# Per-type node sums ahead of the weights, in half blocks, in a graph layer on one core

## The chip, the cores and the metric

The kernel runs on one core of one Trainium2 chip. The metric is the device time of one execution in microseconds (us), and the time given for a kernel is the median of its runs. A core has a matrix engine (TensorE), a vector engine (VectorE), a scalar engine (ScalarE), GpSimd, and SyncE, which here only starts transfers. Each runs its own instruction list in order; semaphores order them against each other.

## The reference

There are 6250 nodes with 128 features, and 100000 edges sorted by destination. Each edge takes its source's row of x through one of two weight matrices, chosen by the edge's type, and the results are summed by destination. A third matrix acts on the node's own row. Then come relu, the residual and a layer norm.

```python
Xs = X[src]
m_data = Xs @ W_data.T + b_data
m_ctrl = Xs @ W_control.T + b_control
msg = jnp.where((edge_types == 0)[:, None], m_data, m_ctrl)
agg = jax.ops.segment_sum(msg, dst, num_segments=X.shape[0])
out = agg + (X @ W_self.T + b_self)
x = _layernorm(x + jax.nn.relu(out), axis=-1)
```

All is fp32. The kernel holds fp32 numbers as three bf16 parts that add up to them, so 128 features are 384 bf16 columns (`D3`).

## The kernel before

**Blocks.** The nodes are cut into 49 blocks of 128 (`NB`). For each block the kernel loads a window of 18 x 128 edges (`KT`, `WIN`), which holds all edges that end in the block. A count of matched edges at the end decides whether a slow general path (`sums_over_all`) has to run; with these inputs it doesn't.

**Messages first.** In a first stage x (transposed, from `in_xt`) is split in three bf16 parts (`split_x`), multiplied by the two type weights (`multiply`, `y`, full-width matmuls), and the fp32 result is split again into three parts: `take` copies a part from the sums to `m3` on ScalarE, `leave` subtracts it on TensorE with minus the unit matrix. `m3` holds 98 tiles of 128 messages, one for each block and type. It stays in the core and is also written to `table` in memory.

**40 packed blocks** in 8 groups of 5 (`GROUPS`) are summed without indirect loads. For a group:

- `edge_fields` computes for each edge its source tile, its place in the tile and its destination; `bucket_hots` makes one-hot rows over the 98 source tiles (`hot_st`); `ranks` counts with `tri` and `rest` matmuls into `acc` and VectorE reductions (`slot`), one step after the other over 18 steps, which of 32 slots (`R`) of its source tile an edge takes.
- `fill_a` and `fill_b` write source and destination of each slot into `small` by matmuls; `fill_c` packs them (`vs`, `packed`) and builds the list of edges that found no slot ("over" to "spilled"), whose messages are fetched with an indirect load (`msg_s`).
- For each block `spread` loads the packed slots to all partitions (`rows`), `select` compares them with the partition number, and `to_hots` makes the one-hot of destinations (`hot_d`).

Then, for each of 25 tiles of four source tiles (`NS`), `gather` runs four matmuls that pick 32 messages each into `g_ps`, `evict` copies them to `gs` on ScalarE, and `add_up` adds them into the block's sum `agg`, again with four matmuls of 32 columns of weights (`by_columns`): each writes its own 32 output partitions. `own_of` adds the node's own term, from x parts that the first stage wrote to memory (`x3_t`) and `load_own` reads back.

**9 gathered blocks** are summed from indirect loads of 128 messages (`gather_rows`, `msg`), 18 per block, beside the packed ones (`gathered_sums`, `agg_g`).

**Behind the sums** `finish_blocks` adds the three parts (`whole`), relu and residual and the statistics, and `normalise` ends a group.

**The order** of all instructions on all engines comes from a planner in the kernel (`Order`): each function is a stream of named steps with an engine, an assumed cost and the steps it needs; `due` gives each a due time, and the planner repeatedly takes the step that can start first, by due time among near ones. The order is then fixed in each engine's instruction list.

Of the kernel before, what the change touches and what calls it, by code (L numbers as in the profile page):

```python
# [26 lines left out]
NT = 2 * NB  # L27
KT = 18
WIN = KT * P
EC = 125  # L30
ER = E // EC
EPS = 1e-05

GROUPS = (5,) * 8
# [6 lines left out]
NS = (NT + 3) // 4  # L41
NC = 4 * NS
# [4 lines left out]
PARTS = (4, 8, 8, 8, 8, 8, 5)  # L47
CH = 6
KC = 6
DC = 13  # L50
# [54 lines left out]
def kernel(  # L105
# [28 lines left out]

    nc = tc.nc
    dram = ctx.enter_context(tc.tile_pool(name="dram", bufs=1, space=DRAM))
    const = ctx.enter_context(tc.tile_pool(name="const", bufs=1))
    table = dram.tile([NT * P, D3], BF16, name="table")
    x3_t = dram.tile([NB, D, 3 * P], BF16, name="x3_t")
    packed = dram.tile([NPB, NT * R], BF16, name="packed")  # L140
    total = const.tile([1, 1], I32, name="total")

    def finish(h, agg, xs):

        nc.vector.scalar_tensor_tensor(h, agg, 0.0, xs, op0=ALU.max, op1=ALU.add)

    def add_parts(agg, work):
        whole = work.tile([P, D], F32, name="whole")
        nc.vector.tensor_reduce(whole, agg.rearrange("p (i c) -> p c i", i=3), axis=AX.X, op=ALU.add)  # L149
        return whole  # L150

    def load_rows(b, work, name="xs", bufs=2):
        xs = work.tile([P, D], F32, name=name, bufs=bufs)
        nc.sync.dma_start(xs, x[b * P : (b + 1) * P, :])
        return xs
# [46 lines left out]
    with ExitStack() as main:  # L202
        sums_over_windows(main, tc, x, xt, edges, w, bias, table, x3_t, packed, total,
                          add_parts, finish, load_rows, norm)

    matched = nc.values_load(total[0:1, 0:1])
    with tc.If(matched != E), ExitStack() as rest:
        sums_over_all(rest, tc, xt, edges, w, bias, table, dram, finish, load_rows, norm)


def sums_over_windows(ctx, tc, x, xt, edges, w, bias, table, x3_t, packed, total,
                      add_parts, finish, load_rows, norm):
# [4 lines left out]
    own_pool = ctx.enter_context(tc.tile_pool(name="own_pool", bufs=1))  # L217
    row_pool = ctx.enter_context(tc.tile_pool(name="row_pool", bufs=RB))
    ps_a = ctx.enter_context(tc.tile_pool(name="ps_a", bufs=1, space=PSUM))
    ctx.enter_context(tc.manual_schedule())  # L220
    stats, root, scale, apply, store_out = norm
    order = Order()
    YB = 4
# [7 lines left out]
    r0 = const.tile([EC, 1], I32, name="r0")  # L231
    nc.sync.dma_start(r0, edges.rearrange("(p k) c -> p (k c)", p=EC)[:, 1:2])
    early = ctx.enter_context(ExitStack())
    build = early.enter_context(tc.tile_pool(name="build", bufs=2))
    ps_y = early.enter_context(tc.tile_pool(name="ps_y", bufs=YB, space=PSUM))
    w_sb = build.tile([D, D3], F32, name="w_sb", bufs=1)
    A.dma_start(w_sb, w)
    b1 = build.tile([1, D3], F32, name="b1", bufs=1)
    A.dma_start(b1, bias)


    iota_f = const.tile([P, 640], F32, name="iota_f")
    G.iota(iota_f, pattern=[[1, 640]], base=0, channel_multiplier=0,
# [4 lines left out]
    base = const.tile([P, NB], I32, name="base")  # L248
    G.iota(base, pattern=[[P, NB]], base=0, channel_multiplier=0)
    counted = {}  # L250
    for n in sorted({DC, CH, *GROUPS}):
        counted[n] = const.tile([P, P, n], BF16, name=f"count{n}")
        G.iota(counted[n], pattern=[[1, P], [0, n]], base=0, channel_multiplier=0,
               allow_small_or_imprecise_dtypes=True)
    bound_p = const.tile([NB, 1], F32, name="bound_p")
    V.tensor_scalar_mul(bound_p, pid[:NB], float(P))
    bound_f = const.tile([EC, NB], F32, name="bound_f")
    V.tensor_scalar_mul(bound_f, iota_f[:EC, :NB], float(P))
    pid1 = const.tile([P, 1], F32, name="pid1")
    V.tensor_scalar_add(pid1, pid, 1.0)  # L260
    slot_f = const.tile([P, R], F32, name="slot_f")
    V.tensor_scalar_add(slot_f, iota_f[:, :R], SLOT)
    ones = const.tile([P, P], F32, name="ones")
# [3 lines left out]
    ident = const.tile([P, P], F32, name="ident")  # L267
    V.tensor_scalar(ident, iota_f[:, :P], pid, None, op0=ALU.is_equal)


    r0f = work.tile([EC, 1], F32, name="r0f")
    V.tensor_copy(r0f, r0)
    begun = work.tile([EC, NB], F32, name="begun")
    V.tensor_scalar(begun, bound_f, r0f, None, op0=ALU.is_gt)
    row_ps = ps_a.tile([P, 512], F32, name="small")
    T.matmul(row_ps[:NB, 0:1], begun, ones[:EC, 0:1], start=True, stop=True)
    row_f = work.tile([NB, 1], F32, name="row_f")
    V.tensor_scalar(row_f, row_ps[:NB, 0:1], -1.0, 0.0, op0=ALU.add, op1=ALU.max)
    row_i = work.tile([NB, 1], I32, name="row_i")
    V.tensor_copy(row_i, row_f)  # L280

    er = build.tile([NB, ER, 3], I32, name="er", bufs=1)
    G.indirect_dma_start(
        out=er.rearrange("p k c -> p (k c)"), out_offset=None,
        in_=edges.rearrange("(p k) c -> p (k c)", p=EC),
# [3 lines left out]
    def three_parts(parts, whole, left):  # L289

        V.tensor_copy(parts[0], whole)
        V.tensor_sub(left, whole, parts[0])
        V.tensor_copy(parts[1], left)
        V.tensor_sub(parts[2], left, parts[1])

    w3 = const.tile([D, 3, D3], BF16, name="w3")
    left = build.tile([D, D3], F32, name="left", bufs=1)
    three_parts([w3[:, i, :] for i in range(3)], w_sb, left)
    order.free["V"] = 7.3


    minus = const.tile([P, P], BF16, name="minus")
    bias3 = const.tile([P, 2 * D], BF16, name="bias3")
# [3 lines left out]
    spill_tiles = [(const.tile([P, Q * P], BF16, name=f"hot_s{i}"),  # L307
                    const.tile([P, D3], BF16, name=f"msg_s{i}")) for i in range(2)]
    hot_b = const.tile([P, P], BF16, name="hot_b")
    msg_b = const.tile([P, D3], BF16, name="msg_b")  # L310
    slot_values = [const.tile([P, (Q + 1) // 2, NC], BF16, name=f"vs{i}") for i in range(2)]
    slot_b = {n: const.tile([P, R, n], BF16, name=f"slot{n}") for n in sorted({*GROUPS})}

    def constants():
        yield step("bias", {"V": 2.4}, ("xr", 0))
        V.memset(bias3, 0.0)
        parts = build.tile([1, 3, D3], BF16, name="parts", bufs=1)
        three_parts([parts[:, i, :] for i in range(3)], b1, left[:1])
        V.tensor_scalar_mul(minus, ident, -1.0)
        yield step("biased", {"A": 1.2}, "bias")  # L320
        for i in range(3):
            A.copy(bias3[32 * i : 32 * i + 1, :], parts[0:1, i, : 2 * D])

        yield step("set", {"V": 4.0}, "bias")
        tri_f = build.tile([P, P], F32, name="tri_f", bufs=1)
        V.tensor_scalar(tri_f, iota_f[:, :P], pid, None, op0=ALU.is_gt)
        V.scalar_tensor_tensor(tri_f, ident, SLOT, tri_f, op0=ALU.mult, op1=ALU.add)
        V.tensor_copy(tri, tri_f)
        V.tensor_scalar(rest, tri_f, -1.0, 1.0, op0=ALU.mult, op1=ALU.add)
        V.tensor_copy(ident_b, ident)  # L330
        for n, tile_n in slot_b.items():
            V.tensor_scalar_add(tile_n, counted[n][:, :R, :], SLOT)


        for vs in slot_values:
            V.memset(vs, 255.0)


        for hot, msg in [*spill_tiles, (hot_b, msg_b)]:
            V.memset(hot, 0.0)  # L340
            V.memset(hot[R : R + 1, :], 1.0)
            V.memset(msg, 0.0)
            V.tensor_copy(msg[R : R + 1, :].rearrange("p (i c) -> p i c", i=3),
                          parts[0:1, :, 2 * D :])

    win, win_g = {}, const.tile([P, NG, KT, 3], I32, name="win_g")
    first = const.tile([1, NB], I32, name="first")
    counts = const.tile([P, NPG + 1], F32, name="counts")
    m3 = const.tile([P, NT, D3], BF16, name="m3")
    m3v = m3.rearrange("p (t b) c -> p t b c", t=2)  # L350

    def starts():
        yield step("er", {"S": 0.0}, lag=15.0)
        yield step("counted", {"V": 1.2}, "er", lag=0.3)
        less = build.tile([NB, ER], BF16, name="less", bufs=1)
        in_row = work.tile([NB, 1], F32, name="in_row")
        V.tensor_scalar(less, er[:, :, 1], bound_p, None, op0=ALU.is_lt, op1=ALU.add,
                        accum_out=in_row)
        first_f = work.tile([NB, 1], F32, name="first_f")
        V.scalar_tensor_tensor(first_f, row_f, float(ER), in_row, op0=ALU.mult, op1=ALU.add)  # L360
        yield step("turned", {"T": 0.6}, "counted")
        first_ps = ps_a.tile([P, 512], F32, name="small")
        T.matmul(first_ps[:1, :NB], first_f, ident[:NB, :NB], start=True, stop=True)
# [32 lines left out]
    def due(kind, *i):  # L396
# [3 lines left out]
        if kind in ("counted", "turned", "first"):  # L400
            return 5.0
# [655 lines left out]
```

## Time and profile before

| | |
|---|---|
| median of 2 runs | 693.0 us (690.38 to 695.63) |
| the profiled execution | 689.8 us, of which its span is 688.1 us |
| TensorE busy, share of the span | 615.4 us, 89% |
| weight loads of TensorE | 527.2 us, 77% |
| VectorE busy | 490.4 us, 71% |
| ScalarE busy | 478.5 us, 70% |
| GpSimd busy | 213.8 us, 31% |
| first gather matmul; last sum ends | 122.1 us; 673.0 us |

In the rows of the profile, `128*32` is the size of the weights (partitions by columns) and `128x384` that of the streamed operand; after the bar stand the busy time, the mean length of one instruction in ns and the idle time before it with what ended it. Narrow matmuls lie beside each other, so their lengths add up to more than the busy time. `PEld` is the weight load. An `L228` line is the helper `by_columns`, whatever tile it works on.

### The profile page before, as it was taken

How to read it: one execution, taken by the hardware profiler on the slowest of the kernel's cores; microseconds unless marked ns; L12 is line 12 of the kernel's file. 1: busy time of each engine (PE TensorE's matmuls, PEld its weight loads, DVE VectorE, ACT ScalarE, POOL GpSimd, SP SyncE). 2: the span in 40 equal slices, each digit the busy share in tenths (PEclk: the TensorE clock that was granted, in tenths of full speed). 3: DMA queues.
4: the chain of work that ended last, by engine and by line, in shares of the span. 5: the costliest groups of instructions: out<-in, count | busy, mean ns of one | idle time of the engine just before them, and what ended most of it. 6: DMA issues, size and time to landing. Idle time of an engine off the chain costs nothing.

```text
span 688.1 us, 29925 instructions
## 1 busy us (share of the span) xinstructions
PE 615.4 (89%) x12874; PEld 527.2 (77%) x12874; DVE 490.4 (71%) x1021; ACT 478.5 (70%) x1140; POOL 213.8 (31%) x181
## 2 busy tenths in 40 slices
PE   1897997899989998899999989999999899998991
PEld 0675774689878887888798877888898778878880
DVE  8684456776787768866887687758975875467863
ACT  2464553677778777787787777887878677767763
POOL 6000000433354333343444342224242433242220
PEclk9999998899999999999999999999999999999996
DMA  2478745441335124432543153325421542144211
GB/s 81 125 213 236 231 141 172 159 150 49 120 104 168 55 66 160 116 99 52 187 116 103 47 182 107 102 62 182 122 88 51 185 116 90 45 161 129 78 31 50
DMA packets 63612, 81.41 MB, mean 118 GB/s; under 512 B 14356, under 2 KB 54815, under 8 KB 63423
## 3 DMA queue, kind: packets, MB, share of 16 engines
q1 hardware_dynamic: 54158, 59.41, 27.1%
q0 software_dynamic: 8160, 16.60, 9.0%
q10 hardware_dynamic: 1154, 3.41, 1.6%
q8 instruction: 102, 1.67, 1.0%
q14 instruction: 38, 0.31, 0.2%
HBM read 61.50 MB, written 17.90 MB: 115 GB/s over the span
## 4 chain that ended last, share of the span: by engine, by line
PE 77%; DMA 7%; DVE 5%; ACT 5%; issue 2%; SPq 1%; ACTq 0%; another core or an unknown queue 0%
PE agg L228 26%; PE g_ps L771 23%; PE acc L228 8%; PE small L623 7%; PE y L480 6%; PE agg_g L228 5%; ACT gs L780 4%; DMA rows<-packed 3%; DMA msg<-table,idx 3%; PE y L500 1%; DVE slot L585 1%; ACT h_p L186 1%; PE y L484 1%; DMA packed<-vs 1%; DMA win<-in_edges 0%
## 5 line engine op out<-in xcount | busy, mean ns | idle before, releaser
L780 ACT CAST gs<-g_ps 128x384 bf16<-128x384 f32 x963 | 397.6, 498 | 128.8 <-PE g_ps L771 86.9
L771 PE MATMUL g_ps<-m,rows 128*32 128x384 bf16 x4000 | 353.6, 331 | 14.1 <-ACT gs L780 8.2
L228 PE MATMUL agg<-gs,hot_d 128*32 128x384 bf16 x4000 | 346.1, 333 | 13.0 <-ACT gs L780 9.5
L866 POOL DMA_INDIRECT msg<-table,idx x162 | 188.4, 1163 | 321.6 <-PE agg_g L228 154.4
L228 PEld LDWEIGHTS <-hot_d 128*32 128x32 bf16 x4000 | 212.2, 137 | 40.9 <-issue 28.9
L771 PEld LDWEIGHTS <-rows 128*32 128x32 bf16 x4000 | 197.7, 136 | 35.3 <-issue 24.4
L585 DVE TENSOR_REDUCE slot<-acc 128x5 bf16<-128x490 f32 x144 | 95.4, 662 | 87.3 <-PE acc L228 56.5
L758 DVE TENSOR_TENSOR hot_d<-count,to 128x1664 bf16<-128x1664 bf16 x80 | 85.0, 1068 | 6.2 <-ACT to L656 4.3
L228 PE MATMUL agg_g<-msg,hot_g 128*32 128x384 bf16 x648 | 68.5, 330 | 5.3 <-DMA msg<-table,idx 5.0
L228 PE MATMUL acc<-hot_st,rest 128*32 128x490 bf16 x544 | 61.2, 377 | 9.0 <-DVE slot L585 8.4
L493 ACT CAST m<-y 128x512 bf16<-128x512 f32 (+1 forms) x75 | 40.7, 580 | 36.2 <-PE y L484 27.3
L228 PE MATMUL acc<-hot_st,tri 128*32 128x490 bf16 x576 | 64.4, 374 | 0.0
L480 PE MATMUL y<-w,x 128*128 128x256 bf16 x441 | 58.4, 289 | 3.6 <-DVE x L464 1.1
L568 DVE TENSOR_TENSOR hot_st<-count,st_b 128x2940 bf16<-128x2940 bf16 x24 | 47.7, 1992 | 12.9 <-PE small L623 11.6
L713 POOL DMA_INDIRECT msg_s<-table,row_i x8 | 14.1, 1760 | 136.8 <-DVE counts L723 109.8
L623 PE MATMUL small<-hot_st,two 128*32 128x98 bf16 x1440 | 55.5, 293 | 0.3 <-DVE two L606 0.3
L480 PEld LDWEIGHTS <-x 128*128 128x128 bf16 x441 | 45.4, 104 | 12.5 <-DVE x L464 1.8
L623 PEld LDWEIGHTS <-two 128*32 128x32 bf16 x1440 | 50.7, 119 | 1.9 <-DVE two L606 0.9
L744 DVE TENSOR_SCALAR rows<-rows,pid 128x3136 bf16<-128x3136 bf16 x40 | 41.6, 1045 | 10.2 <-DMA rows<-packed 10.2
L149 DVE TENSOR_REDUCE whole<-agg 128x128 f32<-128x384 f32 x40 | 22.1, 554 | 28.6 <-PE g_ps L771 16.0
L228 PEld LDWEIGHTS <-hot_g 128*32 128x32 bf16 x648 | 32.1, 124 | 7.9 <-issue 6.3
L228 PEld LDWEIGHTS <-rest 128*32 128x32 bf16 x544 | 23.4, 97 | 19.0 <-issue 17.0
(149 smaller groups left out, 475.9 us busy)
## 6 DMA issues: line engine op xcount, KB each, us to landing
rows<-packed SPq DMA_DIRECT2D x40, 784.0 KB
table<-m SPq DMA_DIRECT2D x10, 768.0 KB
x_p<-x_t SPq DMA_DIRECT2D x40, 96.0 KB
x_t<-x SPq DMA_DIRECT2D x5, 768.0 KB
msg<-table,idx POOLq DMA_INDIRECT x162
xt<-in_xt ACTq DMA_DIRECT2D x5, 512.0 KB
xs_p<-in_x SPq DMA_DIRECT2D x40, 64.0 KB
out<-h_p SPq DMA_DIRECT2D x8, 320.0 KB
```

Source lines behind the costliest of these rows:

```text
L149: nc.vector.tensor_reduce(whole, agg.rearrange("p (i c) -> p c i", i=3), axis=AX.X, op=ALU.add)
L228: T.matmul(out[c : c + 32], lhsT[:, c : c + 32], rhs, **flags)
L480: T.matmul(y[:, j, :], x3s[g][:, b + j - at_part[g], i, :], w3[:, k, : 2 * D], start=i == j == k == 0, stop=False, skip_group_check=True)
L493: A.copy(part_of(b, n, i), ys[b][:, :n, :].rearrange("p b (t c) -> p t b c", t=2))
L568: V.tensor_tensor(hot, counted[n][:, None, 1 : NT + 1, :].to_broadcast([P, KC, NT, n]), fields[grp][2][:, c * KC : c * KC + KC, None, :].t ...
L585: V.tensor_reduce(slots[grp][:, k, :], by_q, axis=AX.X, op=ALU.max)
L623: T.matmul(vt[c0 : c0 + R, q // 2, :], two[:, k, i, :, q], hot[:, k, :, q], start=c == k == 0 and q < 2, stop=c * KC + k == KT - 1, skip_g ...
L744: V.tensor_scalar(rows[b], rows[b], pid1, None, op0=ALU.is_equal)
L758: V.tensor_tensor(hot, counted[DC][:, :, :n], places[grp][:, q, None, c * DC : c * DC + n].to_broadcast([P, P, n]), op=ALU.is_equal)
L771: T.matmul(g_ps[t * R : (t + 1) * R, :D3], rows[b][:, :, s], m3[:, s, :], start=True, stop=True)
L780: (A.copy if e == "A" else V.tensor_copy)(gs, g_tiles.pop((b, g))[:, :D3])
L866: G.indirect_dma_start(out=msgs[j, k], out_offset=None, in_=table[:, :], in_offset=bass.IndirectOffsetOnAxis(ap=idx[:, j, k : k + 1], axis=0),
```

## The change

The weights are taken behind the sum. Since a sum of products with the same matrix is the product of the sum, x itself is summed by destination and by edge type, and only the sums meet the weights, in fp32.

- A block is cut in two **halves of 64 nodes** (`H`), with a window of 9 x 128 edges each. The 128 rows of a half's sum are 64 nodes by two types, so the destination index is the node in the half plus 64 for type 1. The source tiles are now the 49 blocks of x. There are still 25 tiles of four per block: 12 for each half and one shared tile (`mixed`) for source block 48, which also holds the overflow edges of both halves.
- `multiply`, `store_x` and `x3_t` go. x is copied in fp32 to the sums by a unit matrix (`sum_x`) and split in three parts there (`take`, `leave`); `table` has one row per node.
- The sums (`add_up`, `gathered_sums`) are **one matmul with 128 columns of weights** instead of four with 32; a 385th column of ones counts the edges for the bias.
- `behind_sums` is new: per half it adds the three parts, turns the sum by fp32 matmuls with the unit matrix, and per block it multiplies by the weights of both types and adds own term, biases and degrees.
- The groups are 2, 3 and seven times 5 blocks; the counting tiles are written by ScalarE instead of GpSimd; g_ps has 3 banks instead of 4, agg has one for each half; hot_d waits for the overflow list too.

```diff
-KT = 18
+H = P // 2
+NH = 2 * NB
+KT = 9
-GROUPS = (5,) * 8
+GROUPS = (2, 3) + (5,) * 7
+NQ = NB // 4
+NS = 2 * NQ + 1
+SC = NQ + 1
-PARTS = (4, 8, 8, 8, 8, 8, 5)
-CH = 6
-KC = 6
-DC = 13
+PARTS = (4,) * 12 + (1,)
+KC = 3
+EB, GB, MB = 8, 3, 3
...
-    table = dram.tile([NT * P, D3], BF16, name="table")
-    x3_t = dram.tile([NB, D, 3 * P], BF16, name="x3_t")
+    table = dram.tile([NP, D3], BF16, name="table")
...
-        G.iota(counted[n], pattern=[[1, P], [0, n]], base=0, channel_multiplier=0,
-               allow_small_or_imprecise_dtypes=True)
+            yield step(("counts", n), {"A": 0.3 + 0.105 * n})
+            A.copy(counted[n], iota_f[:, :, None].to_broadcast([P, P + 1, n]))
...
+    def sum_x():
+        for g, part in enumerate(parts_of):
+            for j, b in enumerate(range(part.start, part.stop)):
+                yield step(("xp", b), {"T": 0.43}, ("x", g), *([("xl", g - GB)] if g >= GB else []))
+                if j == 0:
+                    sum_ps[g] = ps_g.tile([P, 512], F32, name="g_ps")
+                T.matmul(sum_ps[g][:, j * D : (j + 1) * D], ident, x_sb[:, b, :], start=j == 0,
+                         stop=False, skip_group_check=True)
...
+            for t in range(2, 4) if g == NQ else range(4):
+                h, s = (t - 2, NB - 1) if g == NQ else (g // SC, 4 * (g % SC) + t)
+                T.matmul(g_ps[t * R : (t + 1) * R, :D3], rows[b][:, h, :, s], x3[:, s, :],
+                         start=True, stop=True)
...
-            by_columns(aggs[b], d_hots[b, g // DC][:, :, g % DC], gs_tiles.pop((b, g)),
-                       start=g == 0, stop=False, skip_group_check=True)
-            if g == NS - 1:
-                hot_s, msg_s = spills[grp]
-                by_columns(aggs[b], hot_s[:, q * P : (q + 1) * P], msg_s, start=False, stop=True,
-                           skip_group_check=True)
+                yield step(("s", b, j), {"T": 0.167}, ("e", b, g), ("d", b, h), *free)
+                if j % SC == 0:
+                    aggs[b, h] = ps_a.tile([P, 512], F32, name=f"agg{h}")
+                T.matmul(aggs[b, h][:, : D3 + 1], d_hots[b, h][:, :, c],
+                           gs_tiles[b, g][:, : D3 + 1], start=j % SC == 0, stop=j % SC == SC - 1,
+                           skip_group_check=True)
...
+    def behind_sums(name, blocks, last, h_of):
+        for b in blocks:
+            for h in range(2):
+                yield step(("whole", b, h), {"V": 0.75}, last(b, h), "set3")
+                agg = aggs[b, h]
...
+                V.tensor_reduce(wholes[b][:, h, :], agg[:, :D3].rearrange("p (i c) -> p c i", i=3),
+                                axis=AX.X, op=ALU.add)
+                V.tensor_mul(degs[b][:, h, :], types, agg[:, D3 : D3 + 1].to_broadcast([P, 2]))
+                yield step(("tr", b, h), {"T": 0.5}, ("whole", b, h))
+                by_columns(agg[:, :P], wholes[b][:, h, :], ident, start=True, stop=True,
+                           skip_group_check=True)
+                if h == 1:
+                    yield step(("own", b), {"T": 0.55}, ("tr", b, 1), ("xt", b), "weights", "biased")
+                    y = agg[:, P : 2 * P]
+                    by_columns(y, ones_b, bias3, start=False, stop=False, skip_group_check=True)
+                    by_columns(y, xts.pop(b), w_sb[:, 2 * D :], start=False, stop=False,
+                               skip_group_check=True)
+                yield step(("tc", b, h), {"A": 0.28}, ("tr", b, h), *([("own", b)] if h else []))
...
+                A.copy(a_t[b][:, :, h * H : (h + 1) * H], agg[:, :P].rearrange("p (t n) -> p t n", t=2))
...
+            yield step(("lin", b), {"T": 1.1}, ("tc", b, 0), ("tc", b, 1), ("deg", b))
+            sums = a_t.pop(b)
+            for t in range(2):
+                by_columns(y, sums[:, t, :], w_sb[:, t * D : (t + 1) * D], start=False, stop=t == 1,
+                           skip_group_check=True)
...
+            finish(h, y, deg, b_types, x_sb[:, b, :])
```

`finish` adds bias times degree for both types, then relu and residual as before. In `sums_over_all`, which doesn't run, the same is done in its own way.

## The prediction

> **What bounds the kernel now.** I read the chain of waits, then the groups, then the instructions in order of time in two places. Chain:
>
> ```profile
> PE 77%; DMA 7%; DVE 5%; ACT 5%; issue 2%; SPq 1%; ACTq 0%; another core or an unknown queue 0%
> ```
>
> TensorE carries 77% of the chain. The two groups that fill it, with the eviction between them:
>
> ```profile
> L780 ACT CAST gs<-g_ps 128x384 bf16<-128x384 f32 x963 | 397.6, 498 | 128.8 <-PE g_ps L771 86.9
> L771 PE MATMUL g_ps<-m,rows 128*32 128x384 bf16 x4000 | 353.6, 331 | 14.1 <-ACT gs L780 8.2
> L228 PE MATMUL agg<-gs,hot_d 128*32 128x384 bf16 x4000 | 346.1, 333 | 13.0 <-ACT gs L780 9.5
> ```
>
> ScalarE sat idle 86.9 us waiting for gather results; TensorE waited some 18 us for it. So TensorE's own work sets the pace. What one piece costs is read from start to start, not from durations (331 ns includes latency). TensorE, in the middle of the run:
>
> ```profile
> 225.20 0.39 PE L228 MATMUL agg<-gs,hot_d 128*32 128x384 bf16 x4
> 225.36 0.39 PE L771 MATMUL g_ps<-m,rows 128*32 128x384 bf16 x4
> 225.52 0.39 PE L228 MATMUL agg<-gs,hot_d 128*32 128x384 bf16 x4
> 225.68 0.39 PE L771 MATMUL g_ps<-m,rows 128*32 128x384 bf16 x4
> ```
>
> Four matmuls with 32 columns of weights each run side by side: 0.1625 us for four, whether sum or gather, and nothing is lost between the kinds. Now the build stage, the one place where full-width matmuls (128*128) meet these narrow ones (128*32):
>
> ```profile
> 43.68 0.38 PE L484 MATMUL y<-bias,ones_b 128*128 128x256 bf16 x2
> 43.99 0.39 PE L228 MATMUL acc<-hot_st,rest 128*32 128x490 bf16 x4
> 44.21 0.38 PE L228 MATMUL acc<-hot_st,tri 128*32 128x490 bf16 x4
> 44.52 0.61 PE L500 MATMUL y<-m,minus 128*128 128x256 bf16 x4
> 44.97 0.49 PE L480 MATMUL y<-w,x 128*128 128x256 bf16 x3
> ```
>
> Narrow to narrow: 44.21 - 43.99 = 0.22. Narrow to full: 44.52 - 44.21 = 0.31 for the same work, 0.09 more. Full to full: four in 44.97 - 44.52 = 0.45, so two are 0.22; full to narrow took 43.99 - 43.68 = 0.31 for two, 0.09 more. Every such place between 40 and 107 us shows 0.31 again. **Against the bare stream** (490 columns take 0.204 at the 0.1625 per 384 seen above; 256-column matmuls take 0.109 in the runs of 18) the two changes lose 0.10 and 0.09, plus 0.01 in the group behind each: about 0.11 a change.
>
> The stages: first gather at 122.1 us, last sum ends at 673.0, end at 688.1.
>
> **What the Trainium skill says.** "TensorEngine Tiling (Array Packing)", Key Properties: changing the tiling mode, as against the tile, drains TensorE. It gives no price; the 0.11 us above agrees and is the price. "FP8 and Floating Point Precision", TensorE Precision Notes: true fp32 takes four passes through the array. The trace holds only tiny fp32 matmuls (each recorded as two instructions), so it neither confirms nor refutes the factor. "TensorE: Matmul & The Clock Gate", LDWEIGHTS: load time goes with the columns loaded; the trace has 104 ns for 128 columns, but 97 for 32 contiguous and 137 for 32 strided ones (hot_d), so here the stride shows more than the count.
>
> **The change, part by part.**
>
> *Start.* The 441 matmuls of x by the weights (58.4 us of TensorE), the table's second type and the trip of x3_t through memory go. In place: 49 fp32 copies of x (each 0.43: four passes of 128/2.4 GHz = 0.21, and as much for unhidden weight loads, an estimate) and 25 subtractions, 26 us. VectorE's first two operations took 9.0 and 8.7 us beside GpSimd's 9.1 us of counting; that counting moves to ScalarE, so the first edge row index is ready some 8 us earlier. Group 0 has 2 blocks with 9 rank steps in place of 5 with 18. Before, a step came every 3.25 us (43.99, then 47.24), waiting behind y; with short copies between, I take 1.2. From the trace: window starts known at 27.7 less 10 = 18; four windows at 0.85 and landing, 24; fields 2.4, 27; nine steps 11, 38; selection fill 4, 42; packed, rows, select as before (4.3 + 5.5 + 1.05), 53. First gather at **55** (50 to 65), not 122. The table (4.8 MB instead of 9.6) and x's last part are due by about 45; they hide behind this chain. SP issues 98 window loads instead of 49 and one x load per block instead of two: 0.85 us each, about two per block, inside a block of over 13 us.
>
> *TensorE from the first gather on*, by the built program's order of instructions and the unit costs above: gathers 3920/4 x 0.1625 = 159; sums 1040 x 0.1625 (385 columns, one matmul) = 169; gathered sums 162 x 0.1625 = 26; ranks about half, 27; slot fill 1440 matmuls, 49 columns for 98: 0.036 us each before, 0.025 to 0.036 now, I take 0.030, 43; bias and degree 8; spill lists 9. New fp32 work: per block 5 groups of four narrow matmuls (two turnings, one of own x, two of weights), 245 in all. Floor 0.21 (passes side by side), ceiling 0.85 (one after another); I take 0.43, so 105 (52 to 208). Sum **546**. The same sum for before: 162.5 + 162.5 + 26 + 25 (own) + 7 (spill) + 55 (ranks) + 46 (fill) + 8 = 492, against 551 taken: 59 lost in waits.
>
> *Changes of mode.* In the built order before, TensorE changes between narrow and full width 61 times, 14 of them from the first gather on. After: 2049 and 2014, since the planner sets single full-width sums between narrow gathers (756 times gather to sum, 760 back). 2014 x 0.11 = **222**. Bounds: 0.095 (191) and 0.15 (302), if the strided loads (137 against 97 ns) lie bare as well. At zero the gain case below follows.
>
> *Waits.* agg is split in halves with a bank each, g_ps falls from 4 banks to 3. A g_ps bank is held for about 0.39 + 0.50 + handoffs, 1.05 us: three allow one tile per 0.35, and tiles will come every 0.7. The new chain turn, copy, weights holds agg1 until the block's "sum"; half a block of other sums stands between, some 9 us against 3 to 4 of chain. A group's hot_d now also waits for its overflow list ("listed"), as the list's places go into the same tile; before, the list came within 2 us of it (116.64 against 115.64), so group 0 pays some 2 us, inside the start's range, and later groups are prepared ahead. With TensorE slower, the other engines have more slack; I take 15 of the 59 us of waits (0 to 59).
>
> *VectorE and ScalarE.* VectorE loses 72 rank reductions (48) and half of hot_st (24), gains per block a second reduction (0.55) and eight or so small operations (1.4): 49 x 1.95 = 95. Still about 500 of 850 us: hidden by TensorE. ScalarE loses the y evictions (42), gains 98 copies at 0.3 (29): hidden too. If drains were free this cover still holds: both stay below 80% of 640.
>
> *Tail.* 15.1 plus about 3 for the added chain: 18.
>
> **Sum:** 55 + 546 + 222 + 15 + 18 = 856 span, 1.7 outside it as before (689.8 against 688.1): 858. The profiled run stands 3 us below the median shown (693.0), so **860**.
>
> **Rivals.** *Not slower:* the drain is absorbed because TensorE would wait for ScalarE anyway, or weight loads run ahead through it. Then 55 + 546 + 25 + 18 = 644, 7% faster. It decides below (693 - 644)/2014 = 24 ns a change. For it: ScalarE's idle time shows loose coupling. Against: a dozen places with 0.09 lost and no wait recorded, and TensorE 94% busy in mid-run. *fp32 runs one group after another:* 860 + 103 = about 960. For: no wide fp32 in the trace; against: bf16 narrow matmuls do run side by side. *Strided loads bare:* 860 + 80 = 940. *The change doesn't do what it says:* had the order grouped sums together, the count of changes would show it; it counts 2014.
>
> **Numbers.** Forecast with its own bounds 0.65; costlier fp32 or loads 0.20; drains half price or cheaper but still a loss 0.04; within 2%, 0.03; free drains, faster, 0.08. A measurement of this kernel tells about 2% from no change. The range 760 (860 less 53 for fp32, 31 for drains, 15 for waits) to 940 leaves out the gain case and the far end of fp32.
>
> **What would show it.** Right: the TensorE timeline after shows gather to sum taking about 0.27 instead of 0.16; first gather near 55; blocks every 19 to 20 us instead of 13.8; TensorE on the chain above 80%. Wrong: 0.16 at the changes, or a block period under 15 us, or ScalarE or VectorE leading the chain. A period right but fp32 groups far from 0.43 would mis-size one term only.

## The result, and the profile after

The changed kernel takes 875.1 us (874.27 to 875.98) against 693.0: the ratio is 1.267, with a 95% interval of 1.259 to 1.275. 860 was predicted, in a range of 760 to 940. The profiled execution has a span of 874.2 us. The kernel before was measured again beside the experiments below; it took about 690 us beside some and about 656 beside others, and where it matters the text says which.

The page of the changed kernel: the chain by engine, then the groups that answer to those shown before.

```profile
PE 92%; DVE 2%; DMA 2%; ACT 1%; SPq 1%; issue 1%; another core or an unknown queue 0%; ACTq 0%; DVEq 0%
...
L786 ACT CAST gs<-g_ps 128x384 bf16<-128x384 f32 x935 | 440.5, 480 | 265.5 <-PE g_ps L761 247.9
L761 PE MATMUL g_ps<-x,rows 128*32 128x384 bf16 x3920 | 384.4, 376 | 12.9 <-DVE rows L733 8.1
L804 PE MATMUL agg<-gs,hot_d 128*128 128x385 bf16 x960 | 349.6, 374 | 0.0
```

TensorE went from 77% to 92% of the chain. ScalarE now waits 247.9 us for gathers where it waited 86.9, and TensorE hardly waits in mid-run (0.0 us before the sums, 12.9 before the gathers, 8.1 of them before the very first). Why it is slow although it sums as many tiles as before is seen in its instructions in order of time (start, length, line, output<-inputs, weights, streamed operand):

```profile
304.32 0.38 PE L804 MATMUL agg<-gs,hot_d 128*128 128x385 bf16 x1
304.63 0.39 PE L761 MATMUL g_ps<-x,rows 128*32 128x384 bf16 x4
304.95 0.38 PE L804 MATMUL agg<-gs,hot_d 128*128 128x385 bf16 x1
305.26 0.39 PE L761 MATMUL g_ps<-x,rows 128*32 128x384 bf16 x4
305.59 0.38 PE L804 MATMUL agg<-gs,hot_d 128*128 128x385 bf16 x1
```

A sum and a gather take 305.59 - 304.95 = 0.64 us (0.63 to 0.64 wherever single sums and gathers alternate), where they took 0.325. No row has an idle time behind it: the lost 0.305 us is no wait that the profile knows. The stages: first gather at 61.6 us (122.1 before), last sum ends at 857.8, end at 874.2. A block takes 796.2/40 = 19.9 us instead of 13.8.

### The profile page after: what moved, and what is told of

It is laid out like the page before. It is cut to its first block, busy times and chain, and to the rows that moved or that the text cites. A ratio compares the mean times of both kernels' runs of the same rounds, so it can differ in the third digit from the quotient of the medians.

```text
span 874.2 us, 24607 instructions
## 1 busy us (share of the span) xinstructions
PE 824.6 (94%) x9892; PEld 416.0 (48%) x9892; DVE 509.3 (58%) x1378; ACT 533.4 (61%) x1215; POOL 184.0 (21%) x196
## 4 chain that ended last, share of the span: by engine, by line
PE 92%; DVE 2%; DMA 2%; ACT 1%; SPq 1%; issue 1%; another core or an unknown queue 0%; ACTq 0%; DVEq 0%
PE agg L804 35%; PE g_ps L761 34%; PE agg L224 6%; PE agg_g L940 5%; PE small L610 4%; PE acc L224 4%; PE agg_g L224 1%; PE g_ps L469 1%; PE g_ps L475 1%; DMA win<-in_edges 1%; DMA rows<-packed 1%; DMA r<-in_edges 1%; SPq L376 0%; ACT x L483 0%; ACT gs L786 0%
## 5 line engine op out<-in xcount | busy, mean ns | idle before, releaser
L786 ACT CAST gs<-g_ps 128x384 bf16<-128x384 f32 x935 | 440.5, 480 | 265.5 <-PE g_ps L761 247.9
L761 PE MATMUL g_ps<-x,rows 128*32 128x384 bf16 x3920 | 384.4, 376 | 12.9 <-DVE rows L733 8.1
L804 PE MATMUL agg<-gs,hot_d 128*128 128x385 bf16 x960 | 349.6, 374 | 0.0
L919 POOL DMA_INDIRECT msg<-table,win_g x162 | 171.9, 1061 | 545.7 <-PE agg_g L940 522.5
L761 PEld LDWEIGHTS <-rows 128*32 128x32 bf16 x3920 | 149.8, 138 | 175.5 <-issue 165.9
L804 PEld LDWEIGHTS <-hot_d 128*128 128x128 bf16 x1040 | 140.8, 140 | 176.0 <-issue 172.1
L570 DVE TENSOR_REDUCE slot<-acc 128x10 bf16<-128x490 f32 (+2 forms) x81 | 49.2, 607 | 85.7 <-PE acc L224 82.2
L824 DVE TENSOR_REDUCE whole_p<-agg 128x128 f32<-128x384 f32 x80 | 44.2, 552 | 84.7 <-PE agg L804 84.4
L940 PE MATMUL agg_g<-msg,hot_g 128*128 128x385 bf16 x162 | 55.6, 357 | 0.4 <-DVE hot_g L930 0.4
L610 PE MATMUL small<-hot_st,two 128*32 128x49 bf16 x1440 | 47.1, 272 | 2.3 <-issue 1.3
```

The costliest lines, as they stand in the source:

```text
L570: V.tensor_reduce(slots[grp][:, k, :], by_u, axis=AX.X, op=ALU.max)
L610: T.matmul(vt[c0 : c0 + R, q, :], two[:, k % KC, i, :, 2 * q + h], hot[:, k % KC, :, 2 * q + h], start=k == q == 0, stop=k == KT - 1, skip ...
L761: T.matmul(g_ps[t * R : (t + 1) * R, :D3], rows[b][:, h, :, s], x3[:, s, :], start=True, stop=True)
L786: copy(gs_bufs[n % EB][:, :D3], g_tiles.pop((b, g))[:, :D3])
L804: T.matmul(aggs[b, h][:, : D3 + 1], d_hots[b, h][:, :, c], gs_tiles[b, g][:, : D3 + 1], start=j % SC == 0, stop=j % SC == SC - 1, skip_gro ...
L824: V.tensor_reduce(wholes[b][:, h, :], agg[:, :D3].rearrange("p (i c) -> p c i", i=3), axis=AX.X, op=ALU.add)
```

## The experiments

The numbers of changes of width are counted in each built program's order, from the first gather on. The experiments are called e1 to e12.

### One part undone: narrow sums

```diff
-                T.matmul(aggs[b, h][:, : D3 + 1], d_hots[b, h][:, :, c],
+                by_columns(aggs[b, h][:, : D3 + 1], d_hots[b, h][:, :, c],
...
-            T.matmul(aggs[b, h][:, : D3 + 1], g_hots[j][:, :, k],
+            by_columns(aggs[b, h][:, : D3 + 1], g_hots[j][:, :, k],
```

> The changed kernel with the sums of the packed and of the gathered blocks as four matmuls of 32 columns of weights again; nothing else undone. Changes between narrow and full width from the first gather on fall from 2014 to 16. Theory A (each change of width costs TensorE about 0.15 us, read from the changed kernel: a gather and a sum take 0.63 us against 0.325): 875 less 306 is 569, and up to 60 us of waits come back, so 570 to 630, faster than the kernel before. Rival B (the time lies in the new work behind the sums, the halves or the three banks): still above 690. Rival C (four narrow sums cost TensorE more than one full one): above 800.

Measured (e1): 698.8 us, ratio 1.011 (1.005 to 1.016). Four narrow sums in place of one full one, four times the instructions, save 176 us. The order of time shows why:

```profile
300.99 0.40 PE L761 MATMUL g_ps<-x,rows 128*32 128x384 bf16 x4
301.15 0.40 PE L224 MATMUL agg<-gs,hot_d 128*32 128x385 bf16 x4
301.32 0.40 PE L761 MATMUL g_ps<-x,rows 128*32 128x384 bf16 x4
301.48 0.40 PE L224 MATMUL agg<-gs,hot_d 128*32 128x385 bf16 x4
```

A sum and a gather take 0.33 us again, so rival C falls. Theory A has the mechanism right and the total wrong: 699 lies above its 630. The total is where rival B put it, above 690, so by the total alone the rest of the change could be the cause; e4 below, which has none of that rest, loses 201 us by the width alone. TensorE's loss of some 300 us is gone, but only 176 us of it came back as time. The page of e1 says what took its place:

```profile
PE 55%; DVE 26%; ACT 6%; issue 5%; DMA 5%; SPq 1%; ACTq 0%; DVEq 0%
PE agg L224 21%; PE g_ps L761 20%; DVE hot_g L930 4%; PE small L610 4%; PE acc L224 4%; ACT gs L786 3%; PE agg_g L224 3%; DMA rows<-packed 3%; DVE hot_d L746 3%; DVE h_p L153 2%; DVE slot L570 2%; DVE whole_p L824 2%; PE g_ps L469 2%; DVE rows L733 2%; DVE st L159 1%
```

VectorE, 2% of the chain with full-width sums, carries 26% here. From the first gather (61.0) to the last sum (680.9) are 620 us for some 485 us of TensorE's work (the table further down), so 135 are lost in waits, against 59 in the kernel before and 5 in the changed one.

### Fewer changes with the same sums

Only the gathered blocks' sums at full width:

> Only the 162 sums of the gathered blocks stay at full width. Changes of width: 312. Theory A: the time of the kernel with no full-width sums plus 296 x 0.15 = 45 us, less what hides in waits: 20 to 45 us more than that kernel. Rival (a few changes are hidden, only dense alternation costs): no more than 5 us above it.

Measured (e2): 713.1 us, ratio 1.033 (1.028 to 1.039), 14 us more than with no full-width sum: 0.05 us for each of the 296 changes. It lies between the two expectations. In TensorE's order a gather ahead of a full-width sum still takes 0.32 us there, so TensorE pays the full price; where it has waits anyway, two thirds of that price do not show in the time.

Next, gathers and sums are planned in pairs, so that the same 1202 full-width sums come with half the changes. The edit in `gather` (`add_up` likewise, two sums of one half to a step):

```diff
+            if i % 2:
+                yield step(("g", b, g), {"T": 0.0}, ("g", *tiles[i - 1]))
+                continue
+            two = tiles[i : i + 2]
...
-            yield step(("g", b, g), {"T": 0.165}, ("sel", b), *free, *(last if b == 0 else []))
+            yield step(("g", b, g), {"T": 0.165 * len(two)}, *[("sel", b2) for b2, _ in two], *free,
+                       *(last if b == 0 else []))
```

> The changed kernel with the gathers and the packed sums planned two at a time, all sums still at full width. The same 1202 full-width sums, but 1044 changes of width instead of 2014. Theory A (the price is on the change): 875 less 970 x 0.15 = 730, up to 30 more if three banks of gathers now make TensorE wait: 730 to 760. Rival D (the price is on each full-width sum, whose 128 columns of weights load bare): 860 to 890, as the number of sums is the same.

Measured (e3): 774.3 us, ratio 1.122 (1.117 to 1.128), 14 us above theory A's range and far below rival D's. In TensorE's order:

```profile
302.73 0.55 PE L820 MATMUL agg<-mixed,hot_d 128*128 128x385 bf16 x2
303.11 0.33 PE L820 MATMUL agg<-gs,hot_d 128*128 128x385 bf16 x1
303.27 0.33 PE L956 MATMUL agg_g<-msg,hot_g 128*128 128x385 bf16 x1
303.53 0.56 PE L769 MATMUL g_ps<-x,rows 128*32 128x384 bf16 x8
304.02 0.54 PE L820 MATMUL agg<-gs,hot_d 128*128 128x385 bf16 x2
```

Between full-width sums 303.27 - 303.11 = 0.16 us pass, the bare stream. The rows also show where a change takes its time: the last sum ahead of the gathers takes 303.53 - 303.27 = 0.26, 0.10 more than bare, and the two sums right behind a change take 303.11 - 302.73 = 0.38, 0.05 more than two bare ones. With the number of sums unchanged, 101 us went with the changes: rival D falls, and **the price is on the change of width, not on the full-width sum**. The saving is 0.104 us a change and not 0.15, because some 54 us of waits are back (from the first gather to the last sum 757.9 - 60.5 = 697, less 483 of work and 1044 x 0.153); they are the remainder of this sum.

### One part done alone, in the kernel before

```diff
-            by_columns(aggs[b], d_hots[b, g // DC][:, :, g % DC], gs_tiles.pop((b, g)),
+            T.matmul(aggs[b], d_hots[b, g // DC][:, :, g % DC], gs_tiles.pop((b, g)),
```

> The kernel before with this one part of the change alone: the packed sums as one matmul of 128 columns of weights. Changes of width from the first gather on go from 14 to 1786. Theory A: 693 plus 1772 x 0.15 = 266, less up to 59 us of waits that it covers: 900 to 960. Rival B (the width matters only together with the fp32 work behind the sums): 690 to 720.

Measured (e4): 891.2 us, ratio 1.292 (1.285 to 1.298), 201 us more than the kernel before beside it (689.7). Rival B falls: the width alone, without fp32 weights, halves or three banks, makes more than the whole slowdown. It is 9 us below theory A's 900, with all of the waits covered: 1772 x 0.15 = 266, less the 59 us of waits of the kernel before, is 207. Between 150 and 850 us TensorE is busy for 699 of 700 us there.

And the other part that takes something from the gathers, three banks of g_ps instead of four, in the kernel before:

```diff
-    DB, EB, GB = 4, 8, 4
+    DB, EB, GB = 4, 8, 3
```

> The kernel before with 3 banks of g_ps instead of 4, the one part of the change that takes something from the gathers. The prediction held that three banks allow a tile per 0.35 us and bind nothing at 0.7; here tiles come every 0.55. Theory (banks do not bind): ratio 1.00 to 1.02. Rival (bursts of up to nine sums in a row need the fourth bank): ratio above 1.03.

Measured (e10): 656.4 us, ratio 0.999 (0.996 to 1.002), beside a kernel before of 657. Three banks do not bind there.

### What a change costs: the layout of the weights

> The changed kernel, sums at full width, with hot_d laid out so that the 128 columns of weights of a sum lie one behind the other instead of 13 elements apart; 2014 changes of width as before. In the changed kernel a change costs 0.153 us, not the 0.11 read before. Theory S (the surplus of 0.04 is the sum's strided weights, loaded bare after a change): about 1000 sums x 0.04 to 0.08 less, 795 to 835. Theory R (the surplus lies with the gather's weights, rows, 49 elements apart: the first gather behind a sum takes 0.22 us where another takes 0.1625): 870 to 880, no difference.

> As the run before, and the selected rows are also written so that the 32 columns of weights of a gather lie one behind the other. Theory R: a pair of changes falls from 0.305 to about 0.21 us (0.10 and 0.09 and 0.01 as in the build stage of the kernel before), 1000 x 0.095 = 95 less: 780. Theory S: the same as the run before. A third theory (the surplus has nothing to do with strides): 875 in both runs. If VectorE's selection, which now writes with a stride, takes 3 us instead of 1.04, it still has room: 58% busy.

```diff
-            d_hots[b, h] = hot = work.tile([P, P, SC], BF16, name="hot_d", bufs=DB)
+            hot = work.tile([P, SC, P], BF16, name="hot_d", bufs=DB)
+            d_hots[b, h] = hot = hot.rearrange("p c n -> p n c")
...
-            V.tensor_scalar(rows[b], rows[b], pid1, None, op0=ALU.is_equal)
+            picked = work.tile([P, 2, NB, R], BF16, name="picked", bufs=RB)
+            picked = picked.rearrange("p h s r -> p h r s")
+            V.tensor_scalar(picked, rows[b], pid1, None, op0=ALU.is_equal)
+            rows[b] = picked
```

The first edit (hot_d) is in both runs, the second (`picked`) in e6 alone. Both miss every total that was expected, with 1229 us (e5) and 1438 us (e6), since VectorE became the bound: it carries 57% and 66% of their chains. Writing with a stride, it took 7.6 us for a hot_d (1.08 before) and 7.4 for a selection (1.04). But the price can be read where TensorE runs without a wait. In both stretches shown the granted clock was 1.00, as in the changed kernel's (over these whole runs it was 0.79 and 0.75). Contiguous sum weights (e5), then contiguous sum and gather weights (e6):

```profile
408.47 0.34 PE L805 MATMUL agg<-gs,hot_d 128*128 128x385 bf16 x1
408.74 0.39 PE L762 MATMUL g_ps<-x,rows 128*32 128x384 bf16 x4
409.06 0.34 PE L805 MATMUL agg<-gs,hot_d 128*128 128x385 bf16 x1
```

```profile
506.64 0.34 PE L808 MATMUL agg<-gs,hot_d 128*128 128x385 bf16 x1
506.91 0.35 PE L765 MATMUL g_ps<-x,picked 128*32 128x384 bf16 x4
507.19 0.34 PE L808 MATMUL agg<-gs,hot_d 128*128 128x385 bf16 x1
```

A pair takes 0.59, then 0.55 us, so it loses 0.265, then 0.22: 0.133 and 0.11 a change, from 0.153. Theories S and R are each right for about half of the surplus, and the third falls. The recorded weight loads got shorter by the same 0.04 us: 140 to 100 ns for a sum's in e5, and 138 to 99 ns for a gather's in e6. With no stride anywhere the price is the 0.11 us that the prediction had read in the build stage, where all weights were contiguous.

### Where the gain of the rest went

With narrow sums the rest of the change starts the gathers 61 us earlier and yet gains nothing. Two edits on that kernel (e1's). First, hot_g reads its operand without a stride:

```diff
-    dest_g = const.tile([P, KT, 2 * NG], BF16, name="dest_g")
+    dest_g = const.tile([P, 2 * NG, KT], BF16, name="dest_g")
...
-                            dest_g[:, None, :, j].to_broadcast([P, P, KT]), op=ALU.is_equal)
+                            dest_g[:, j, None, :].to_broadcast([P, P, KT]), op=ALU.is_equal)
```

> The kernel with narrow sums (699 us) and one more edit: dest_g is laid out so that hot_g reads its second operand without a stride. hot_g took 2.28 us for 1152 elements where hot_d takes 1.08 for 1664, and the planner books 0.73. Theory V (without the changes of width VectorE in its fixed order is late for TensorE, and hot_g, 4% or 28 us of the chain, is the largest single piece): 665 to 685. Rival P (three banks of g_ps and the eviction bound it): 695 to 702.

Then the planner's costs as well, two of six shown:

```diff
-                yield step(("tr", b, h), {"T": 0.5}, ("whole", b, h))
+                yield step(("tr", b, h), {"T": 0.22}, ("whole", b, h))
...
-            yield step(("lin", b), {"T": 1.1}, ("tc", b, 0), ("tc", b, 1), ("deg", b))
+            yield step(("lin", b), {"T": 0.55}, ("tc", b, 0), ("tc", b, 1), ("deg", b))
```

> As the run before, and the planner's assumed costs set to what the trace of the changed kernel shows: turning 0.22 us instead of 0.5, own term 0.28 instead of 0.55, weights 0.55 instead of 1.1, slot fill 0.092 n instead of 0.116 n, the last step 1.65 instead of 1.4, eviction 0.42 instead of 0.37. Only the order of instructions changes. Theory O (the order was made for costs that are not so, and engines wait for each other in it): 10 to 30 us less than the run before. Rival P: within 5 us of it.

Measured, beside a kernel before of 656.0: 635.5 us (e7), ratio 0.971 (0.967 to 0.975), and 607.9 us (e8), ratio **0.930** (0.924 to 0.936). The last is faster than both kernels. hot_g fell from 2.33 to 0.82 us. From e7 to e8 nothing but the planned order changed (and with it the engine of six evictions), for 27.5 us: theory O holds, and rival P falls, as e8 keeps the three banks and evictions. The chains by engine, e7 and then e8:

```profile
PE 48%; DVE 31%; DMA 10%; issue 5%; ACT 4%; SPq 1%; ACTq 0%; DVEq 0%
PE 68%; DVE 9%; DMA 8%; ACT 6%; SPq 4%; issue 3%; ACTq 0%; DVEq 0%
```

In e7, with hot_g already short, VectorE still carries 31% of the chain (26% in e1); only the new order of e8 takes it down to 9%, and there from first gather to last sum (59.7 to 586.6) some 42 us are lost in waits. How much of the step from e1's 1.011 to 0.971 is hot_g's is not shown: e1 ran beside a kernel before of 690, e7 beside one of 656. So theory V is not shown either.

The same two edits with full-width sums:

> The changed kernel with its full-width sums, and the two edits of the fastest kernel so far (hot_g without a stride, the planner's costs set to the trace): 2016 changes of width. With narrow sums these two edits took the ratio to the kernel before from 1.011 to 0.930. Theory A (with full-width sums TensorE is never idle from the first gather on, so what VectorE and the order cost is covered): ratio 1.24 to 1.28, as without them (1.267). Rival (their gain of 8% comes on top, whatever the width): ratio 1.15 to 1.20.

Measured (e9): 864.5 us, ratio 1.316 (1.307 to 1.325) where the kernel before took 657. Both expected ratios are missed, because they were reckoned for a kernel before of 690. In time it is 10 to 13 us below the two measurements of the changed kernel beside 693, where a gain of 8% would be 70, so the rival falls: TensorE's changes of width cover nearly all that these edits mend. The changed kernel itself was never measured beside a kernel before of 656.

> The changed kernel itself, once more, beside e12. The kernel before took 690 us on the chips of some calls and 656 on those of others. Theory A (with full-width sums TensorE works without a gap, and what differs between chips lies in the waits): 865 to 880 on either kind of chip, so a ratio near 1.27 where the kernel before takes 690 and near 1.33 where it takes 656. Rival (a chip is quicker as a whole): ratio 1.26 to 1.28 on either.

> The kernel with narrow sums alone once more, on the same chip as e11: it had a ratio of 1.011 where the kernel before takes 690. Theory (its waits shrink on the quicker kind of chip as those of the kernel before do): where that takes 656, 655 to 670, ratio 1.00 to 1.02; on the other kind 699 again. Rival (its waits are of its own order): 690 to 700 on either kind.

Measured: 877.7 us (e11), ratio 1.266 (1.260 to 1.272), and 700.7 us (e12), ratio 1.013 (1.008 to 1.018). The kernel before took 693 here, so both repeat what was known and decide nothing about the quicker case. The expectations speak of two kinds of chip; that is not shown, since the record has the same chip number for e9 and e10, beside 657, and for these two, beside 693. What makes the difference stays open.

## Why the prediction was right

Its mechanism is shown: e3 and e4 tie the loss to the change of width, and e1 removes it. That its total came as close as 2% is luck: two mis-sized terms, 63 us too much work and 86 us too little for the changes, nearly cancel.

| term | predicted, us | in the profile after, us |
|---|---|---|
| first gather | 55 | 61.6 |
| TensorE's own work from there | 546 | 483 |
| 2014 changes of width | 222 (0.11 each) | 308 (0.153 each) |
| waits | 15 | 5 |
| tail | 18 | 16.4 |
| span | 856 | 874.2 |

**Changes of width.** The mechanism, the count and the place were right. The unit was read in the build stage, whose weights are contiguous, while the weights of sums and gathers are strided. The bound of 0.15, "if the strided loads lie bare as well", is what came; e5 and e6 show the stride as the cause of the surplus. So a gather ahead of a sum takes 304.95 - 304.63 = 0.32 us and not the 0.27 that was given as a sign. (The bare stream of 490 columns is 0.207 at the rate named there, not 0.204; the 0.11 stands with either. Of the places between 40 and 107 us most show 0.31, a few up to 0.34, and at 56.7 a wait for VectorE lies in between.)

**fp32.** A group of four narrow fp32 matmuls takes 0.215 us, the floor of the range, where 0.43 was taken. The slot fill is read from the first two of these rows:

```profile
312.35 0.65 PE L610 MATMUL small<-hot_st,two 128*32 128x49 bf16 x20
312.80 0.42 PE L224 MATMUL agg<-ident,whole_p 128*32 128x128 f32 x8
...
315.82 0.61 PE L224 MATMUL agg<-w_sb,a_t_p 128*32 128x128 f32 x16
316.25 0.17 PE L852 MATMUL agg<-deg_p,nodes 128*32 128x4 bf16 x4
```

Sixteen recorded instructions are two groups of four matmuls, two for each, and take 316.25 - 315.82 = 0.43 us. That is what four passes take at the bf16 rate (4 x 128 columns at 0.1625 us for 384 are 0.217), so the unhidden weight loads that the prediction added did not come, and 245 groups cost 53 us and not 105. The slot fill took 0.0225 us a matmul (twenty in 312.80 - 312.35 = 0.45) instead of 0.030, 11 us less. Together: 546 - 52 - 11 = 483.

**Waits.** The 5 us are what is left of the 796.2 us, not a measured wait. That TensorE, when slower, leaves slack to all others held, and e9 confirms it.

**Start.** The chain was right up to the slots (packed at about 44 us instead of 42). Then the step that was costed at nothing failed, SP's 98 window loads, "inside a block of over 13 us". SP's queue in the changed kernel:

```profile
43.57 3.19 SPq L380 DMA_DIRECT2D win_g<-in_edges  x4
46.85 0.38 SPq L489 DMA_DIRECT2D table<-x  x1
47.72 1.53 SPq L380 DMA_DIRECT2D win_g<-in_edges  x2
49.35 0.38 SPq L489 DMA_DIRECT2D table<-x  x1
50.23 0.33 SPq L380 DMA_DIRECT2D win_g<-in_edges  x1
50.66 1.93 SPq L625 DMA_DIRECT2D packed<-vs  x2
```

ScalarE had written vs by 43.9 us. Its transfer left at 50.7, behind seven window loads of the gathered blocks and two table writes. These 6.8 us are about the 6.6 by which the first gather came late. This is read from the trace; that the loads caused the delay is not shown, as no run moved them.

**The rivals.** "Not slower" fell: the drain is not absorbed where TensorE has no slack. Its number was wrong too. It gave 644 us with 25 us of waits; e1, with 16 changes left, took 699 with 135. So even free changes would not have made this change, in its planned order, faster than a kernel before of 690, and the break-even of 24 ns a change did not exist. The prediction's claim that VectorE and ScalarE stay hidden holds only under full-width sums. "fp32 one group after another" is refuted by the rows above; "strided loads bare" was right and hidden in the total by the cheaper fp32; that the change doesn't do what it says is refuted by the 0.64 us rows.

## What to carry to other kernels

Look in the built order for places where TensorE goes from narrow to full-width weights and back: each cost 0.11 us with contiguous and 0.153 us with strided weights, shown as no wait at all, so matmuls that alternate like these belong in one width even if that means four times the instructions. Read such a price where the operands lie as they will in the new place, stride included. And when one engine is made the sole bound, the waits that it covers are no saving later: taking 300 us off TensorE gave 176 us, and a gain on the kernel before (ratio 0.971, then 0.930) came only with hot_g's stride and then the planner's costs mended as well.

## What the runs showed of the hardware that was not expected

- VectorE writing bf16 with a stride of 128 elements took 7.6 us for 1664 elements per partition, against 1.08 us; a selection of 3136 elements with a stride of 32 took 7.4 us against 1.04. Reading one operand with a stride of 18 took 2.33 us for 1152 elements, against 0.82.
- In e5 and e6, the runs with those strided writes, GpSimd's indirect gathers (`msg`) got longer too, 2.7 and 3.6 us on average instead of 1.06. Those that ran beside one of the long VectorE instructions took 5.8 us (e5) and 6.5 us (e6) in the median, the others 0.95.
- Narrow fp32 matmuls run side by side in groups of four: 0.215 us for 128 columns, four times the bf16 rate.
- Recorded bf16 weight loads depended on the stride and not on the number of columns: 100 ns for 128 contiguous columns and 99 for 32 (e6), 140 and 138 for strided ones (the changed kernel).
